# Making gathered columns on VectorE alone instead of on VectorE and ScalarE: a graph attention kernel on one core

## The chip, the core and the metric

The kernel runs on one core of one Trainium2 chip. A core has TensorE (PE; its weight loads are shown apart, as PEld), VectorE (DVE), ScalarE (ACT), GpSimd (POOL) and SyncE (SP), which run their own instruction streams and meet at semaphores, and 16 DMA engines that serve the queues of all of them. The metric is the device time of one execution in microseconds; the lower the better. The time before is the median of three runs, 2430.73 us.

## The reference

A graph layer with 6250 nodes, 206250 edges sorted by destination, width 128 and 8 heads of 16, then a residual and a layer norm:

```python
Qh = (h @ WQ).reshape(N, H, D)
Kh = (h @ WK).reshape(N, H, D)
Vh = (h @ WV).reshape(N, H, D)
Eh = (edge_attr @ WE).reshape(-1, H, D)
score = jnp.einsum('ehd,ehd,ehd->eh', Kh[src], Qh[dst], Eh) * inv_sqrt_d
score = jnp.exp(jnp.clip(score, -5.0, 5.0))
msg = Vh[src] * score[:, :, None]
wV = jax.ops.segment_sum(msg, dst, num_segments=N)
Z = jax.ops.segment_sum(score, dst, num_segments=N)
h_out = wV / (Z[:, :, None] + 1e-06)
...
x = _layernorm(x + h_out, axis=-1)
```

The sources of the edges are random nodes, so the rows `Kh[src]`, `Vh[src]` have to be fetched row by row. The destinations are sorted, so neighbouring edges add into neighbouring nodes.

## The kernel before

The edges are cut into 1612 tiles of 128, and the tiles into 406 batches of four (the last few of two or one). A table `kv` of the K and V rows of all nodes is computed once and stored in HBM; x itself lies transposed in SBUF (`xT_sb`, a feature per partition and a node per column), interleaved with a zero behind each node in `xz`.

For each batch the loop does, spread over some five iterations:

- `gather`: POOL fetches the K and V rows of a tile's 128 sources with one indirect DMA per tile (line 463), into `kvrows`. The first gather of a batch waits for the qps of an earlier batch, twelve batches back at first and three later on (`lag`).
- `stage_a`: TensorE makes Q rows of the destinations (`qps`, line 560, from a one-hot matrix) and the edge features (`eps`, line 565).
- `products` and `scores`: VectorE multiplies `kvrows` by `qps` (line 572) and by `eps` (line 574), and sums by head (lines 581, 584).
- `weigh` and `messages`: ScalarE takes the exponentials (lines 590, 592), and VectorE multiplies the V rows by them (line 623).
- `stage_0`, `stage_0t` with `mark`, `mark_t`: TensorE and ScalarE build the one-hot matrices of the destinations (`marks`, lines 508 and 529; `marks_t`, lines 542 and 551).
- `stage_c`: TensorE adds the messages by destination (`agg`, line 645); `finish` and `layernorm` finish blocks of nodes when all their edges are in. `q_rows` (lines 313 to 320) builds the table of Q rows a little ahead of its use.

Not every tile is gathered. In 169 batches the last of the four tiles is made another way: the 128 source columns of x are copied from `xT_sb` into a tile `xcol` in SBUF, one by one, at addresses that are read into registers 16 at a time (`addresses`, line 389); then TensorE multiplies `xcol` by the K and V weights (`colkv`, line 445), and ScalarE puts the result into `kvrows` (line 452). `gather` leaves these tiles out. Which batches have such a tile is fixed by `COL0` and `COLP`: from batch 26 on, five in eleven.

The copies of a tile are shared. ScalarE makes the first 58 of the 128 columns, one per instruction (line 421). VectorE makes the other `COLV` = 70, two per instruction (line 418): it reads eight bytes at each of two places, where one pair is (column, zero) and the other (zero, column), and joins them with a bitwise or. The copies are spread evenly over the batches, eight batches ahead of their use (`due`, `COLL`). VectorE's come in runs of eight instructions, at two places of a batch (`run`), with two halves between which other small work is put; ScalarE's come all in one place, after `place_columns`, and ahead of `mark` and `mark_t` (`columns`).

The part of the loop in which the engines' orders are fixed (lines of the order in one iteration):

```python
place_columns()
if 0 <= b - 1 < nbat:
    stage_0(b - 1)
if b + 2 < nbat:
    stage_0t(b + 2)
if b < nbat:
    columns(b)
mark(b - 1)
if b + 2 < nbat:
    mark_t(b + 2)
```

All instructions of an engine run in the order in which the program issues them. `marks`, `qrows`, `colkv` and the sums of `finish` share two PSUM buffers; `marks_t`, `qps` and `eps` have one each.

Of the kernel before, what the change touches and what calls it, by code (L numbers as in the profile page):

```python
# [8 lines left out]
F32 = mybir.dt.float32  # L9
I32 = mybir.dt.int32  # L10
# [15 lines left out]
LEFT, RIGHT = 1, 1  # L26
# [24 lines left out]
QLOOK = 3  # L51
QREG = 16
COL0 = 26
COLP = (11,5)
COLN = 16
COLV = 70
COLL = 8
RING = 4096
MR = 3 * WT + 2
# [2 lines left out]
XT_AT = RING + P  # L62
# [21 lines left out]
def col_runs(v):  # L84

    n = len(column_tiles()) * (P - COLV, COLV)[v]
    return -(-n // (COLN * P))


def column_runs(srcT, v):  # L90

    import numpy as np
    cols = srcT.reshape(NT, P)[column_tiles()]
    cols = (cols[:, :P - COLV], cols[:, P - COLV:])[v].ravel()
    runs = np.zeros((col_runs(v) * P, COLN), cols.dtype)
    runs.ravel()[:len(cols)] = cols
    return np.ascontiguousarray(runs.reshape(col_runs(v), P, COLN).transpose(1, 0, 2).reshape(P, -1))


def pair_of(t):  # L100
# [14 lines left out]
def q_built(j):  # L115

    return min(NB, (j * N // NJ + 3 * P - 1) // P)


@with_exitstack  # L120
def edge_attention(ctx: ExitStack, tc: tile.TileContext, x, xT, srcT, srcA, srcV, dstT, dstB, dst0, bnd, loB, onB, onQ, eaT,
                   wq, wkv, we, out, kv, qtab, qs, relD, relO):
    nc = tc.nc
    cp = ctx.enter_context(tc.tile_pool(name="const", bufs=1))
# [25 lines left out]
    batches = cut_batches()  # L150
    nbat = len(batches)
    col_batches = [t // B for t in column_tiles()]
    col_at = [cp.tile([P, col_runs(v), COLN], I32, name=f"col_at{v}") for v in range(2)]

    def src_col(t):
        return src_sb[0][:, t:t + 1] if t < C0 else src_sb[1][:, t - C0:t - C0 + 1]

    with ExitStack() as fast:
# [225 lines left out]
        def addresses(v):  # L384

            while len(ahead[v]) < 2 and read[v] < len(col_batches) * share[v]:
                r = read[v] // COLN
                read[v] += COLN
                ahead[v].append(nc.values_load_multi_w_load_instructions(  # L389
                    col_at[v][r % P:r % P + 1, r // P],  # L390
                    engines=((mybir.EngineType.Activation, mybir.EngineType.DVE)[v],),
                    min_val=XT_AT + 8 * LEFT - 4, max_val=XT_AT + 8 * (LEFT + N - 1),
                    skip_runtime_bounds_check_because="edges name nodes")[1])

        def column(at, n, dt):
# [3 lines left out]
            return xz_bytes[:, ds(at - XT_AT, n)].bitcast(dt)  # L399
# [6 lines left out]
        def copy(v):  # L406

            c, (k, i) = copied[v] % COLN, divmod(copied[v], share[v])
            if c == 0:
                addresses(v)  # L410
                at_hand[v] = ahead[v].pop(0)
            copied[v] += 1 + v
            if k not in col_tiles:
                col_tiles[k] = wp.tile([P, P], F32, name="xcol", bufs=6)
            to, at = col_tiles[k], at_hand[v]
            if v:
                i += share[0]
                nc.vector.tensor_tensor(to.bitcast(I32)[:, i:i + 2], column(at[c], 8, I32),  # L418
                                        column(at[c + 1], 8, I32), op=ALU.bitwise_or)
            else:  # L420
                nc.scalar.copy(to[:, i:i + 1], column(at[c], 4, F32))  # L421
# [95 lines left out]
        def mark(b):  # L517

            if b not in marks:
                return  # L520
            m, oh, h, n, k = marks.pop(b)
            base = oh[:, h, :n, HW * h:HW * h + HW]
            if k == 2:
                (p_, *dims) = [list(x) for x in base.ap]
                base = bass.AP(tensor=base.tensor, offset=base.offset, ap=[p_, [B * P + HW, 2], *dims])
                m = m.rearrange("p (k b) w -> p k b w", k=2)
            else:
                m = m[:, :n]
            nc.scalar.activation(base, m, AF.Relu)  # L529
# [3 lines left out]
        def stage_0t(b):  # L533

            if b in marks_t or b in ohTs:
                return
            t0, n = batches[b][0], len(batches[b])
            m = psM.tile([QROWS, B * P], F32, name="marks_t")
            for i in range(0, n * P, WT * P - t0 % WT * P):
                e0 = (t0 * P + i) % (WT * P)  # L540
                w = min(n * P - i, WT * P - e0)
                nc.tensor.matmul(m[:, i:i + w], steps_q, rels[(t0 * P + i) // (WT * P)][:, e0:e0 + w], start=True, stop=True)  # L542
            marks_t[b] = m, n
# [154 lines left out]
        for b in range(nbat + 4):  # L698
# [41 lines left out]
            for _ in run(b, 0.5) if on else ():  # L740
                fill(False)
# [3 lines left out]
            for _ in run(b, 1.0) if on else ():  # L745
                fill()
# [225 lines left out]
```

## Time and profile before

| | |
|---|---|
| median of three runs | 2430.73 us (2430.68 to 2443.36) |
| the profiled execution | 2453.43 us, of which its span 2451.6 us |
| mean granted TensorE clock | 0.771 |
| DMA | 329.11 MB, mean 134 GB/s |
| gathers in the trace (line 463) | 1395 from `kv`, 48 from x |
| column copies in the trace | ScalarE 9802, VectorE 5915 |

The profile page shows one execution. In its groups of instructions each row has the line, the engine, the operation, what is written and read, the count, then the busy time and the mean of one in ns, and then the idle time of the engine ahead of them with what ended most of it. "issue" is idle time for which the profile shows no cause, "remote" a release whose origin it doesn't show. In a timeline each row has the start, the duration, the engine and line, the count of merged instructions, and in brackets the idle time ahead of it. Spans on POOL are rough by the page's own words, and the ends of matmuls are modelled.

### The profile page before, as it was taken

The page shows a single profiled execution, that of the slowest core. Times are in us where ns is not written, and L with a number is a line of the kernel's source. Part 1 is how long each engine was busy: PE and PEld are TensorE (multiplying, and loading weights), DVE is VectorE, ACT ScalarE, POOL GpSimd, SP SyncE. Part 2 cuts the span into 40 slices and gives each one's busy share as a digit, 9 for nine tenths or more (in the row PEclk, how much of TensorE's full clock was granted, in tenths as well). Part 3 has the DMA queues.
Part 4 walks back from the last instruction along what each step waited for, and adds up shares of the span by engine and source line. Part 5 has one row for each costly group of instructions (what it writes and reads, how often), then busy time and mean ns, then how long its engine had stood idle before and what let it go on. Part 6 is the DMA issues. An engine that isn't in the chain of part 4 may idle for free.

```text
span 2451.6 us, 47432 instructions
## 1 busy us (share of the span) xinstructions
PE 1827.4 (75%) x10000; PEld 1470.7 (60%) x10000; DVE 1672.0 (68%) x8773; ACT 1567.2 (64%) x11614; POOL 1377.3 (56%) x1450
## 2 busy tenths in 40 slices
PE   5786677777777778688777777777777777767786
PEld 3565555655556656566556666666655656556565
DVE  3455676676677767677767677777677777676765
ACT  2334666666677767676766766767676766666752
POOL 6554555555555555555655555655555655555563
PEclk7777777687788877777878777877777877777877
DMA  6544444344344444444444444544444444445442
GB/s 201 183 140 120 120 123 125 112 145 130 111 138 146 129 123 149 120 138 130 149 133 130 142 145 123 153 134 127 138 139 125 138 138 132 144 120 149 136 130 62
DMA packets 165518, 329.11 MB, mean 134 GB/s; under 512 B 65389, under 2 KB 90929, under 8 KB 165221
## 3 DMA queue, kind: packets, MB, share of 16 engines
q0 software_dynamic: 68480, 186.02, 26.1%
q1 hardware_dynamic: 95617, 139.22, 18.1%
q14 instruction: 217, 1.78, 0.2%
q8 instruction: 80, 1.31, 0.2%
q10 hardware_dynamic: 1124, 0.79, 0.1%
HBM read 309.01 MB, written 16.88 MB: 133 GB/s over the span
## 4 chain that ended last, share of the span: by engine, by line
PE 29%; ACT 24%; DVE 18%; issue 13%; another core or an unknown queue 7%; DVEq 4%; ACTq 2%; DMA 1%; POOL 0%; SPq 0%; POOLq 0%
ACT xcol L421 16%; PE eps L565 8%; PE agg L645 7%; DVE xcol L418 5%; DVEq L389 4%; DVE kq L574 3%; DVE kq L572 3%; PE finps L604 3%; ACT onehotT L551 3%; PE marks_t L542 3%; PE qps L560 2%; DVE sc L581 2%; ACT onehot L529 2%; DVE msg L623 2%
## 5 line engine op out<-in xcount | busy, mean ns | idle before, releaser
L463 POOL DMA_INDIRECT kvrows<-kv,src x1395 | 1326.5, 951 | 1032.2 <-issue 334.2
L421 ACT COPY xcol<-xz 128x1 f32 x9802 | 1046.2, 189 | 401.7 <-issue 389.9
L645 PEld LDWEIGHTS agg<-msg,onehot 128*128 128x128 f32 x3224 | 529.4, 241 | 382.5 <-issue 220.4
L565 PE MATMUL eps<-we_sb,ea 128*128 128x128 f32 x3224 | 592.3, 341 | 216.5 <-DVE kq L574 181.9
L565 PEld LDWEIGHTS eps<-we_sb,ea 128*128 128x128 f32 x3224 | 519.8, 244 | 249.2 <-DVE kq L574 205.3
L645 PE MATMUL agg<-msg,onehot 128*128 128x136 f32 x3224 | 621.2, 349 | 26.9 <-DVE msg L623 8.4
L418 DVE TENSOR_TENSOR xcol<-xz 128x2 int32 x5915 | 508.8, 152 | 143.8 <-issue 139.7
L574 DVE TENSOR_TENSOR kq<-kq,eps 128x512 f32<-128x512 f32 x406 | 272.4, 671 | 295.3 <-remote 177.8
L572 DVE TENSOR_TENSOR kq<-kvrows,qps 128x512 f32<-128x512 f32 x406 | 275.4, 678 | 184.8 <-PE qps L560 46.2
L542 PE MATMUL marks_t<-rows_q,steps_q 5*126 5x512 bf16 x406 | 190.4, 469 | 228.1 <-ACT onehotT L551 79.3
L623 DVE TENSOR_TENSOR msg<-kvrows,exp_p 128x512 f32<-128x512 f32 x406 | 273.1, 673 | 10.4 <-ACT exp_p L590 8.3
L581 DVE TENSOR_REDUCE sc<-kq 128x32 f32<-128x512 f32 x406 | 272.4, 671 | 0.3
L551 ACT ACTIVATE onehotT<-marks_t 126x512 bf16<-126x512 f32 x406 | 237.1, 584 | 46.2 <-remote 22.2
L590 ACT ACTIVATE exp_p<-sc 128x32 f32<-128x32 f32 x406 | 81.8, 202 | 238.6 <-DVE msg L623 105.0
L560 PE MATMUL qps<-qw,onehotT 126*128 126x128 bf16 x1612 | 194.5, 254 | 21.2 <-DVE kq L572 13.9
L560 PEld LDWEIGHTS <-onehotT 126*128 126x128 bf16 x1612 | 155.9, 117 | 71.4 <-issue 43.7
L604 PEld LDWEIGHTS finps<-sum,shift 128*128 128x128 f32 x640 | 116.8, 270 | 57.8 <-issue 24.7
L445 PE MATMUL colkv<-wkv_sb,xcol 128*128 128x256 f32 x338 | 136.1, 494 | 18.9 <-ACT onehot L529 10.4
L604 PE MATMUL finps<-sum,shift 128*128 128x136 f32 x640 | 129.5, 376 | 11.4 <-remote 6.7
L529 ACT ACTIVATE onehot<-marks 128x512 f32<-128x512 f32 (+2 forms) x206 | 119.4, 580 | 15.2 <-issue 6.4
L592 ACT ACTIVATE msg<-sc 128x32 f32<-128x32 f32 x406 | 88.1, 217 | 6.1 <-issue 6.0
L508 PE MATMUL marks<-steps,rows 26*128 26x512 bf16 (+2 forms) x206 | 91.9, 446 | 0.0
(86 smaller groups left out, 822.1 us busy)
## 6 DMA issues: line engine op xcount, KB each, us to landing
ea<-eaT SPq DMA_DIRECT2D x201, 512.0 KB
kvrows<-kv,src POOLq DMA_INDIRECT x1395
qw<-qs SPq DMA_DIRECT2D x202, 31.5 KB
kv<-ea SPq DMA_DIRECT2D x12, 512.0 KB
qs<-qst SPq DMA_DIRECT2D x48, 96.0 KB
rows_q<-relD SPq DMA_DIRECT2D x202, 6.0 KB
rows<-relO SPq DMA_DIRECT2D x202, 6.0 KB
xb<-x SPq DMA_DIRECT2D x24, 128.0 KB
```

The lines of the kernel that those rows point to most:

```text
L418: nc.vector.tensor_tensor(to.bitcast(I32)[:, i:i + 2], column(at[c], 8, I32), column(at[c + 1], 8, I32), op=ALU.bitwise_or)
L421: nc.scalar.copy(to[:, i:i + 1], column(at[c], 4, F32))
L463: ins = nc.gpsimd.indirect_dma_start(out=g[:k, i, :f], out_offset=None, in_=rows, in_offset=bass.IndirectOffsetOnAxis(ap=src_col(t)[:k], a ...
L551: nc.scalar.activation(ohTs[b][:, :n * P], m[:, :n * P], AF.Relu)
L560: expanded[b] = nc.tensor.matmul(pq[:, i, :], ohT[:, i * P:i * P + P], loaded[t0 // WT], start=True, stop=True)
L565: nc.tensor.matmul(pe[:, i, :], ea[:, i * P:i * P + P], we_sb, start=True, stop=True)
L572: nc.vector.tensor_tensor(t0[:, :n], g[:, :n, :D], pq[:, :n], op=ALU.mult)
L574: nc.vector.tensor_tensor(t0[:, :n], t0[:, :n], pe[:, :n], op=ALU.mult)
L581: nc.vector.tensor_reduce(sc[:, :n], t0[:, :n].rearrange("p b (h d) -> p b h d", h=H), axis=AX.X, op=ALU.add)
L604: nc.tensor.matmul(ps, shift[:, P - s:2 * P - s], sums[k // 2][:, k % 2], start=first and i == 0, stop=stop and i == len(parts) - 1)
L623: nc.vector.tensor_tensor(m[:, :n, :D].rearrange("p b (h d) -> p b h d", h=H), g[:, :n, D:].rearrange("p b (h d) -> p b h d", h=H), exp_p[ ...
L645: nc.tensor.matmul(aggs[u][:, 0 if final else k % 2], oh[:, i, :], m[:, i, :], start=not final and t % (2 * G) == 0, stop=tail)
```

## The change

ScalarE copies no columns any more. VectorE makes all 128 columns of a tile, two per instruction as before, and there are 83 such tiles instead of 169 (`COLP` is 9 and 2: two batches in nine). So 86 tiles more are gathered by POOL. There is one table of addresses instead of two, `columns` and its call are gone, and `due` and `run` count the columns of whole tiles. The order of everything else in the loop is the same.

```diff
-COLP = (11,5)
+COLP = (9, 2)
 COLN = 16
-COLV = 70
 COLL = 8
...
-        copied, projected = [0, 0], []
-        share = [P - COLV, COLV]
-        ahead, read, at_hand = [[], []], [0, 0], [None, None]
+        copied, projected = [0], []
+        total = len(col_batches) * P
+        ahead, read, at_hand = [], [0], [None]
...
-        def due(b, v, part):
-
-            n = int((b + part - 1 - COL0 + COLL) * COLP[1] * share[v] / COLP[0] + 1e-6) // (1 + v) * (1 + v)
-            return min(n, len(col_batches) * share[v])
+        def due(b, part):
+
+            return min(int((b + part - 1 - COL0 + COLL) * COLP[1] * P / COLP[0] + 1e-6) // 2 * 2, total)
...
-            if v:
-                i += share[0]
-                nc.vector.tensor_tensor(to.bitcast(I32)[:, i:i + 2], column(at[c], 8, I32),
-                                        column(at[c + 1], 8, I32), op=ALU.bitwise_or)
-            else:
-                nc.scalar.copy(to[:, i:i + 1], column(at[c], 4, F32))
-
-        def columns(b, part=1.0):
-
-            while copied[0] < due(b, 0, part):
-                copy(0)
+            at = at_hand[0]
+            nc.vector.tensor_tensor(col_tiles[k].bitcast(I32)[:, i:i + 2], column(at[c]),
+                                    column(at[c + 1]), op=ALU.bitwise_or)
 
         def run(b, part):
 
-            left = due(b, 1, part) - copied[1]
-            if left >= COLN // 2 or 0 < left == len(col_batches) * share[1] - copied[1]:
+            left = due(b, part) - copied[0]
+            if left >= COLN // 2 or 0 < left == total - copied[0]:
                 for i in range(COLN // 2):
                     if i == COLN // 4:
                         yield
-                    if copied[1] < len(col_batches) * share[1]:
-                        copy(1)
+                    if copied[0] < total:
+                        copy()
...
-        for v in range(2):
-            nc.sync.dma_start(col_at[v], (srcA, srcV)[v].rearrange("p (r c) -> p r c", c=COLN))
-            nc.vector.tensor_scalar(col_at[v], col_at[v], 8, XT_AT + 8 * LEFT, op0=ALU.mult, op1=ALU.add)
-        odd = col_at[1].rearrange("p r (c z) -> p (r c) z", z=2)[:, :, 1]
+        nc.sync.dma_start(col_at, srcC.rearrange("p (r c) -> p r c", c=COLN))
+        nc.vector.tensor_scalar(col_at, col_at, 8, XT_AT + 8 * LEFT, op0=ALU.mult, op1=ALU.add)
+        odd = col_at.rearrange("p r (c z) -> p (r c) z", z=2)[:, :, 1]
...
-            if b < nbat:
-                columns(b)
             mark(b - 1)
```

More of the change, by code (lines that the diff above doesn't have):

```diff
@@ L81, in column_tiles, with col_runs, column_runs @@
     return [batches[b][-1] for b in at if b < len(batches) and batches[b][-1] < NT - TAIL - 4 * B]
[L84 to L90, printed above, removed]
+def col_runs():
+    return -(-len(column_tiles()) // COLN)
+def column_runs(srcT):
     import numpy as np
-    cols = srcT.reshape(NT, P)[column_tiles()]
-    cols = (cols[:, :P - COLV], cols[:, P - COLV:])[v].ravel()
-    runs = np.zeros((col_runs(v) * P, COLN), cols.dtype)
+    cols = srcT.reshape(NT, P)[column_tiles()].ravel()
+    runs = np.zeros((col_runs() * P, COLN), cols.dtype)
     runs.ravel()[:len(cols)] = cols
-    return np.ascontiguousarray(runs.reshape(col_runs(v), P, COLN).transpose(1, 0, 2).reshape(P, -1))
+    return np.ascontiguousarray(runs.reshape(col_runs(), P, COLN).transpose(1, 0, 2).reshape(P, -1))
 def pair_of(t):
@@ L152, in edge_attention @@
     col_batches = [t // B for t in column_tiles()]
-    col_at = [cp.tile([P, col_runs(v), COLN], I32, name=f"col_at{v}") for v in range(2)]
+    col_at = cp.tile([P, col_runs(), COLN], I32, name="col_at")
     def src_col(t):
@@ L378, in edge_attention @@
         used = [0]
-        copied, projected = [0, 0], []
-        share = [P - COLV, COLV]
-        ahead, read, at_hand = [[], []], [0, 0], [None, None]
[L384 to L391, printed above, removed]
+        copied, projected = [0], []
@@ L392, in addresses, with column @@
+        total = len(col_batches) * P
+        ahead, read, at_hand = [], [0], [None]
+        def addresses():
+            while len(ahead) < 2 and read[0] < total:
+                r = read[0] // COLN
+                read[0] += COLN
+                ahead.append(nc.values_load_multi_w_load_instructions(
+                    col_at[r % P:r % P + 1, r // P], engines=(mybir.EngineType.DVE,),
                     min_val=XT_AT + 8 * LEFT - 4, max_val=XT_AT + 8 * (LEFT + N - 1),
                     skip_runtime_bounds_check_because="edges name nodes")[1])
-        def column(at, n, dt):
+        def column(at):
@@ L397, in column @@
             at = at.with_bounds(min_val=XT_AT + 8 * LEFT - 4, max_val=XT_AT + 8 * (LEFT + N - 1),
                                 guaranteed_mod_val=0, out_of_modulus=4)
-            return xz_bytes[:, ds(at - XT_AT, n)].bitcast(dt)
-        def due(b, v, part):
-            n = int((b + part - 1 - COL0 + COLL) * COLP[1] * share[v] / COLP[0] + 1e-6) // (1 + v) * (1 + v)
-            return min(n, len(col_batches) * share[v])
-        def copy(v):
-            c, (k, i) = copied[v] % COLN, divmod(copied[v], share[v])
+            return xz_bytes[:, ds(at - XT_AT, 8)].bitcast(I32)
@@ L409, in copy @@
+        def due(b, part):
+            return min(int((b + part - 1 - COL0 + COLL) * COLP[1] * P / COLP[0] + 1e-6) // 2 * 2, total)
+        def copy():
+            c, (k, i) = copied[0] % COLN, divmod(copied[0], P)
             if c == 0:
-                addresses(v)
-                at_hand[v] = ahead[v].pop(0)
-            copied[v] += 1 + v
+                addresses()
+                at_hand[0] = ahead.pop(0)
+            copied[0] += 2
             if k not in col_tiles:
                 col_tiles[k] = wp.tile([P, P], F32, name="xcol", bufs=6)
-            to, at = col_tiles[k], at_hand[v]
@@ L941 @@
         "srcT": np.ascontiguousarray(srcT.reshape(NT, P).T),
-        "srcA": column_runs(srcT, 0),
-        "srcV": column_runs(srcT, 1),
+        "srcC": column_runs(srcT),
         "dstT": np.ascontiguousarray(dstT.reshape(NT, P).T),
```

2 lines of the change are left out of this document (1 added, 1 removed).

## The prediction

> **What bounds the kernel now.** I read the page first, for the shares of the engines, the chain of work and the costliest groups.
>
> ```profile
> span 2451.6 us, 47432 instructions
> ...
> PE 1827.4 (75%) x10000; PEld 1470.7 (60%) x10000; DVE 1672.0 (68%) x8773; ACT 1567.2 (64%) x11614; POOL 1377.3 (56%) x1450
> ...
> PE 29%; ACT 24%; DVE 18%; issue 13%; another core or an unknown queue 7%; DVEq 4%; ACTq 2%; DMA 1%; POOL 0%; SPq 0%; POOLq 0%
> ...
> L463 POOL DMA_INDIRECT kvrows<-kv,src x1395 | 1326.5, 951 | 1032.2 <-issue 334.2
> L421 ACT COPY xcol<-xz 128x1 f32 x9802 | 1046.2, 189 | 401.7 <-issue 389.9
> ...
> L418 DVE TENSOR_TENSOR xcol<-xz 128x2 int32 x5915 | 508.8, 152 | 143.8 <-issue 139.7
> ...
> L445 PE MATMUL colkv<-wkv_sb,xcol 128*128 128x256 f32 x338 | 136.1, 494 | 18.9 <-ACT onehot L529 10.4
> ```
>
> The view of line 463 adds the gathers from x, ahead of the table kv.
>
> ```profile
> L463 POOL DMA_INDIRECT kvrows<-x,src x48: 939/945/2613, 3.7 to 71.2; - x48
> ```
>
> No engine is full, POOL is not on the chain that ended last, and it looks idle for 44% of the span: a gather shows 951 ns, and mostly some 0.3 us of issue before the next. The timeline of POOL alone says otherwise. I take it at the end, where no column is copied any more (ScalarE's last copy starts at 2376.2, VectorE's at 2372.4).
>
> ```profile
> L421 ACT COPY xcol<-xz x9802: 173/187/213, 202.4 to 2376.2; 128x1 f32 x197
> ...
> L418 DVE TENSOR_TENSOR xcol<-xz x5915: 118/151/235, 196.7 to 2372.4; 128x2 int32 x198
> ```
>
> ```profile
> 2377.03 0.95 POOL L463 DMA_INDIRECT kvrows<-kv,src  x1 [2.01 <-PE qps L560]
> ...
> 2383.04 0.95 POOL L463 DMA_INDIRECT kvrows<-kv,src  x1 [1.31 <-PE marks_t L542]
> ...
> 2393.37 0.94 POOL L463 DMA_INDIRECT kvrows<-kv,src  x1 [1.88 <-remote]
> ...
> 2405.18 0.94 POOL L463 DMA_INDIRECT kvrows<-kv,src  x1 [2.08 <-PE marks_t L542]
> ```
>
> The same in stretches (stretch, length, POOL's busy time in gathers and their number, granted clock, DMA share, GB/s):
>
> ```profile
> 2377.00:2419.90 42.90, 27.46 (x29) 0.82 0.36 103
> 200.00:2377.00 2177.00, 1229.67 (x1295) 0.77 0.45 133
> ```
>
> Between the starts shown POOL makes 4, 7 and 8 gathers, back to back. The runs take 6.01, 10.33 and 11.81 us from start to start, and the idle time behind them grows with their length: 1.31, 1.88, 2.08 us. A wait for another engine would not grow with the number of gathers; work of POOL that goes on behind the recorded end of the instruction would. So a gather costs POOL 42.90/29 = **1.48 us**, not 1.25. From 200 to 2377 us, where columns are copied, POOL issues 1295 gathers in 2177 us, 1.68 us each. At 1.48 they would take 1917 us: POOL's own work is 88% of that stretch, and 260 us are waits of POOL for the loop.
>
> Next, who holds the loop up. Each gather group waits for a qps of TensorE some batches back, so I read a long POOL wait with all engines.
>
> ```profile
> 1384.38 0.69 DVE L574 TENSOR_TENSOR kq<-kq,eps 128x512 f32<-128x512 f32 x1 [1.95 <-remote]
> ...
> 1384.66 0.95 POOL L463 DMA_INDIRECT kvrows<-kv,src  x1 [0.30 <-issue]
> ...
> 1385.78 0.19 ACT L421 COPY xcol<-xz 128x1 f32 x1 [0.52 <-issue]
> 1386.49 0.19 ACT L421 COPY xcol<-xz 128x1 f32 x1 [0.52 <-issue]
> 1387.20 1.58 ACT L421 COPY xcol<-xz 128x1 f32 x15 [0.51 <-issue]
> 1388.68 0.59 ACT L529 ACTIVATE onehot<-marks 128x512 f32<-128x512 f32 x1
> ...
> 1389.32 0.80 PE L313 MATMUL qrows<-wq_sb,xz 128*128 128x128 f32 x2 [3.76 <-ACT onehot L529]
> ...
> 1389.91 0.63 PE L560 MATMUL qps<-qw,onehotT 126*128 126x128 bf16 x4
> ...
> 1390.82 0.94 POOL L463 DMA_INDIRECT kvrows<-kv,src  x1 [5.21 <-PE qps L560]
> ```
>
> Another one, where a run of gathers holds the others up:
>
> ```profile
> 1734.29 1.16 PE L565 MATMUL eps<-we_sb,ea 128*128 128x128 f32 x8
> ...
> 1740.02 0.95 POOL L463 DMA_INDIRECT kvrows<-kv,src  x1 [0.30 <-issue]
> ...
> 1741.13 0.69 DVE L574 TENSOR_TENSOR kq<-kq,eps 128x512 f32<-128x512 f32 x1 [3.87 <-remote]
> ```
>
> Late in a run of gathers ScalarE's copies, else about 0.1 us apart, come one or two per 0.7 us, and engines resume together as the run ends: L574 of VectorE, whose eps TensorE issued from 1734.29 on, waits 3.87 us until 1741.13, just behind the recorded end of that run's last gather (1740.02 + 0.95). So the loop advances mostly at the start of a run and after it. In the first of the two waits the last gather ends at 1385.61; of the 5.21 us that follow, 1.88 are POOL's own (the run of 7 above), and 3.3 are excess. In those, ScalarE first works off its 15 remaining copies (1387.20 to 1388.68, 1.5 us); only then come onehot, qrows, qps and the gather.
>
> So POOL's gathers set the pace, and ScalarE's copies are a part, not all, of what POOL waits for on top.
>
> **The change part by part.**
>
> *Gathers.* 1612 tiles less 169 are the 1395 + 48 gathers of the trace; less 83 they are 1529, so **86 more**. The steps between the runs above give (10.33 - 6.01)/3 = 1.44 and 11.81 - 10.33 = 1.48 us for one more in a run; I take 1.47: 86 x 1.47 = **+126 us**. Bounds: below, 86 x 1.25 = 107 us, which is nothing if it fits into POOL's waits (a rival); above, 86 x 1.68 = +145 us, if the loop's waits grow in step. Nothing covers this term, since POOL has no spare time at 1.48 us. The added bytes are 6% of queue 0's, and the DMA engines are 45% busy in the stretch; I cost them at nothing.
>
> The Trainium skill (Perfetto Trace Analysis, section DMA Instruction — SWDGE (GPSIMD)) says that the profile's end of such an instruction is the moment when the last DSP has finished generating descriptors. By that rule POOL is free 0.95 us after a start, and the growing idle time would be other engines' doing; the rows above speak against it.
>
> *ScalarE's columns.* 9802 copies go, 1046.2 us busy and 401.7 us of idle before them, with ScalarE's register loads; of that only what POOL's waits contain comes back. Who waits for ScalarE is in the waits of TensorE:
>
> ```profile
> PE marks_t L542 <- ACT onehotT L551: 79.3, 55, 7.8
> ...
> PE marks_t L542 <- ACT exp_p L590: 28.3, 27, 2.0
> PE marks_t L542 <- ACT kvrows L452: 26.8, 15, 3.5
> ...
>   ACT onehot L529: 65.1, 25
> ```
>
> (the last: idle time before qrows, L313, of loads and matmuls together, so about half of it counts once). 79.3 + 28.3 + 26.8 + 33 = 167 us is what TensorE waits for a ScalarE that is behind, and is my upper bound of the gain: some of it lies under POOL's own 88%. The lower bound is nothing. In the wait shown ScalarE has 1.5 of 3.3 us; in others the chain runs through VectorE's msg or a half-clock agg, and copies lie beside it. I take a third of 260 us: **-87 us**. What is late next is VectorE's chain L574, L581, its column run, L584, L623, which stays as it is.
>
> *VectorE's columns.* 83 x 64 = 5312 instructions for 5915, 603 fewer at (508.8 + 139.7)/5915 = 110 ns: 66 us of VectorE's time. Per batch it makes 128 x 2/9 = 28 columns where it made 70 x 5/11 = 32. VectorE sits on POOL's path only in the excess, 260 of 2177 us, an eighth: -8 us, within the rounding of the term above, so not added. The cover is POOL; without it the whole 66 us would count.
>
> The Trainium skill (SBUF — State Buffer, section Who interferes with whom) says that a VectorE instruction with two SBUF inputs contends with a GpSimd instruction that reads SBUF; such are these column instructions, so 603 fewer might shorten gathers. A gather lasts 0.94 to 0.95 us in the rows with columns and without, so I give it nothing.
>
> *Projections.* 86 pairs of colkv go, 136.1 x 86/169 = 69 us of TensorE, and 86 copies L452; like VectorE's, they count in the excess alone, an eighth, and are left in the rounding. The address table is one short load and one multiply less at the start: nothing, beside the first gathers.
>
> *Sum.* +126 - 87 = **+39 us**. The profiled execution took 2453.4 us (span 2451.6), 0.9% over the median of 2430.7; the difference carries over, so 2430.7 + 39 = **2470 us**.
>
> **The rivals.**
>
> *Faster: the loop catches up.* ScalarE's backlog is the main cause of POOL's excess, and without it the loop always has its qps ready. At the end of the span, without any columns, three runs go at POOL's own price. If TensorE's whole 167 us come back, 2430.7 + 126 - 167 = **2390 us**; with all 260 us of waits gone 2297, the extreme. It decides from the point where more than 126 us are saved, half of POOL's excess. For it: the wait shown. Against it: VectorE still makes 14 column instructions a batch, and longer runs hold the loop up for longer.
>
> *Full price: nothing comes back.* Longer runs of POOL hold the others up as much as ScalarE's absence helps: +145, **2576 us**. For it: the runs of seven are the ones with the long waits behind them, and four-gather batches become the rule (323 of 406, before 237).
>
> *The gathers are hidden and the loop is the bound*, as POOL's 56% and its 0% of the chain suggest; then the change does not cost what it adds, and 167 us come off: **2264 us**. POOL at 1.25 us a gather would be busy for 1529 x 1.25 = 1911 us only. (The rule of the Trainium skill on the profile's end, above, would have it so.) Against it: the 4, 7, 8 pattern.
>
> That the change doesn't do what it says is excluded by the counts: nothing else makes columns.
>
> **How the numbers follow.** Less than 0.5%, 12 us, is about what a measurement of this kernel can't tell from no change. Forecast (between +12 and +110 us) 0.53; full price (above +110) 0.14; the two sides cancel within 12 us 0.10; faster, loop catches up 0.20; gathers hidden 0.03. So slower 0.67, same 0.10, faster 0.23. The range leaves out the hidden gathers, the outer part of the rival of catching up and that of the full price: 2375 to 2565.
>
> **What would show it.** In the changed kernel's page: 1481 gathers on L463 from kv; no L421-like copies on ScalarE, and ScalarE busy for some 1567 - 1046 = 521 us. If the first step is right, POOL's runs of 4 take about 6.0 us from start to start, and the mean per gather in the long stretch lies between 1.48 and 1.68 us; I expect about 1.60. If it falls to 1.48, the faster rival holds; if it stays at 1.68, the full price. If runs of 4 come closer than 5.6 us, POOL's own price is wrong. If waits for ScalarE vanish from marks_t and qrows while POOL's mean stays, the second step is wrong: VectorE or the hold-up itself sets the excess.

## The result, and the profile after

Before takes 2448.45 us and after 2426.59 us, medians of 20 runs each taken side by side (2429.1 to 2466.73, and 2414.82 to 2439.95). The ratio is 0.9919, 95% interval 0.9894 to 0.9943: after is some 20 us faster. Forecast were 2470 us, 39 us slower than before; the range of 2375 to 2565 us holds the time, the sign does not hold.

Of the seven lots of runs below, the first two had every execution of every kernel some 20% shorter, before's own too (medians of 1887.94 and 1889.46 us), so each ratio is taken to before in the same lot; the result and the other five lots have before at 2417 to 2467 us. I call them the short and the long lots and come back to them at the end.

The page of after: the busy times of the engines, the chain that ended last, and the two groups that grew or shrank.

```profile
span 2419.9 us, 35774 instructions
...
PE 1823.0 (75%) x9828; PEld 1470.2 (61%) x9828; DVE 1637.7 (68%) x8169; ACT 580.7 (24%) x1726; POOL 1458.4 (60%) x1536
...
PE 9%; DVE 6%; issue 3%; another core or an unknown queue 1%; DVEq 1%; POOL 0%; DMA 0%; SPq 0%; ACT 0%; POOLq 0%; ACTq 0%
...
L449 POOL DMA_INDIRECT kvrows<-kv,src x1481 | 1408.3, 951 | 920.1 <-issue 359.8
...
L411 DVE TENSOR_TENSOR xcol<-xz 128x2 int32 x5312 | 467.5, 154 | 133.4 <-issue 126.2
```

The 86 gathers are there (1481 for 1395), ScalarE's 9802 copies are gone (ACT 580.7 us busy for 1567.2; 521 were forecast), and yet POOL sits idle less than before: 920.1 us ahead of its gathers where it was 1032.2. The chain is followed back over only a fifth of the span here and carries nothing. In the view of groups most of TensorE's waits for ScalarE have gone as well. marks_t, which waited 79.3 us for ScalarE's onehotT, waits 3.8 us:

```profile
L528 PE MATMUL marks_t<-rows_q,steps_q 5*126 5x512 bf16 x406 | 196.9, 485 | 21.5 <-issue 14.8 <-ACT onehotT L537 3.8 <-DMA rows<-relO 2.7
```

The same stretch as in the prediction, POOL alone (stretch, length, busy time and number of gathers, granted clock, DMA share, GB/s):

```profile
200.00:2377.00 2177.00, 1334.20 (x1406) 0.74 0.47 140
```

That is 2177/1406 = 1.55 us for a gather, where 1.68 were before and 1.60 forecast. By the prediction's own price of 1.48, POOL's waits for the loop would have shrunk from 260 to 96 us: 164 us would have come back, not 87. The experiments show that this way of dividing the time was itself wrong.

**A way to divide it that the experiments bear out.** Between two gathers of a run POOL is idle for 0.305 us (0.30 or 0.31 in the timelines; 451.2/1481 in a run of the second lot below that has no longer pauses). So I take the idle time that the group's row gives, less 0.305 us for each gather, and call the rest the gaps: before 1032.2 - 1395 x 0.305 = 607 us, after 920.1 - 1481 x 0.305 = 468 us. At 0.951 + 0.305 = 1.256 us, 86 gathers are +108 us; the gaps are -138 us; the sum of -30 us is, but for 2 us, the difference of the two spans, 2451.6 and 2419.9. That alone is bookkeeping; that 1.256 us is what a gather costs, and that the gaps belong to the loop, is for the runs to show.

### The profile page after: what moved, and what is told of

Its sections match the earlier page's. It is cut to its first block, busy times and chain, and to the rows that moved or that the text cites. A ratio compares the mean times of both kernels' runs of the same rounds, so it can differ in the third digit from the quotient of the medians.

```text
span 2419.9 us, 35774 instructions
## 1 busy us (share of the span) xinstructions
PE 1823.0 (75%) x9828; PEld 1470.2 (61%) x9828; DVE 1637.7 (68%) x8169; ACT 580.7 (24%) x1726; POOL 1458.4 (60%) x1536
## 3 DMA queue, kind: packets, MB, share of 16 engines
q0 software_dynamic: 72608, 197.30, 27.7%
## 5 line engine op out<-in xcount | busy, mean ns | idle before, releaser
L449 POOL DMA_INDIRECT kvrows<-kv,src x1481 | 1408.3, 951 | 920.1 <-issue 359.8
L551 PE MATMUL eps<-we_sb,ea 128*128 128x128 f32 x3224 | 622.2, 352 | 299.0 <-DVE kq L560 182.2
L551 PEld LDWEIGHTS eps<-we_sb,ea 128*128 128x128 f32 x3224 | 541.8, 253 | 344.7 <-DVE kq L560 207.2
L631 PE MATMUL agg<-msg,onehot 128*128 128x136 f32 x3224 | 634.6, 354 | 107.4 <-DVE msg L609 47.8
L631 PEld LDWEIGHTS agg<-msg,onehot 128*128 128x128 f32 x3224 | 540.4, 245 | 276.3 <-DVE msg L609 92.8
L411 DVE TENSOR_TENSOR xcol<-xz 128x2 int32 x5312 | 467.5, 154 | 133.4 <-issue 126.2
L528 PE MATMUL marks_t<-rows_q,steps_q 5*126 5x512 bf16 x406 | 196.9, 485 | 21.5 <-issue 14.8
L494 PE MATMUL marks<-steps,rows 26*128 26x512 bf16 (+2 forms) x206 | 98.6, 479 | 0.0
L314 DVE CAST qst<-qrows 128x128 bf16<-128x128 f32 (+1 forms) x49 | 14.2, 290 | 116.6 <-remote 67.8
L570 DVE TENSOR_SCALAR sc<-sc 128x32 f32<-128x32 f32 x406 | 76.6, 189 | 15.4 <-remote 6.6
```

What stands on the lines that cost most here:

```text
L411: nc.vector.tensor_tensor(col_tiles[k].bitcast(I32)[:, i:i + 2], column(at[c]), column(at[c + 1]), op=ALU.bitwise_or)
L449: ins = nc.gpsimd.indirect_dma_start(out=g[:k, i, :f], out_offset=None, in_=rows, in_offset=bass.IndirectOffsetOnAxis(ap=src_col(t)[:k], a ...
L551: nc.tensor.matmul(pe[:, i, :], ea[:, i * P:i * P + P], we_sb, start=True, stop=True)
L631: nc.tensor.matmul(aggs[u][:, 0 if final else k % 2], oh[:, i, :], m[:, i, :], start=not final and t % (2 * G) == 0, stop=tail)
```

## The experiments

Two theories stood at the start. **A**: gathers set the pace, and ScalarE's column copies made a good part of POOL's waits. **B**: the gathers are covered, and after is faster because an engine of the loop has less to do. Within A, **A1** blames the place of the copies in ScalarE's queue, **A2** their load. **C**, added later: what is held up during runs of gathers makes the waits, whatever ScalarE does. Some expectations speak of two kinds of chip; but by the records the same chip ran the first lot, a short one, and the fifth, a long one.

### First lot (short): four changes

One column tile in place of 83:

```diff
-    return [batches[b][-1] for b in at if b < len(batches) and batches[b][-1] < NT - TAIL - 4 * B]
+    return [batches[b][-1] for b in at if b < len(batches) and batches[b][-1] < NT - TAIL - 4 * B][:1]
```

> After with one column tile instead of 83: 82 more tiles are gathered (1563) and VectorE loses almost all its column copies. Theory A (POOL's queue of gathers sets the time: gathers x 1.48 us and the waits of POOL for the loop on top): 82 x 1.48 = 121 us more POOL work; of after's 95 us of waits some more may go, since VectorE is freed too. So 40 to 121 us over after, i.e. +1% to +4% against the kernel before. Theory B (the gathers are covered, the loop's engines set the time, and after is faster because an engine of the loop has less to do): no slower than after, 1% faster than before or better.

Before, with one wide copy for ScalarE's 58 of a tile:

```diff
-            if c == 0:
+            if c == 0 and v:
...
-            else:
-                nc.scalar.copy(to[:, i:i + 1], column(at[c], 4, F32))
+            elif i == 0:
+                nc.scalar.copy(to[:, :share[0]], xT_sb[:, LEFT:LEFT + share[0]])
```

> Before, with ScalarE's 58 copies of one column per tile replaced by one copy of 58 neighbouring columns (58 columns of each of the 169 tiles are then not those of the edges), without the address loads of ScalarE. The 169 tiles stay, 1395 gathers stay. Theory A: the gathers' own 1395 x 1.48 us stay, and the waits of POOL for the loop fall from 260 us to after's level of 95 us: about 165 us faster, -5.5% to -7.5%. Theory B (gathers covered, ScalarE's load alone is what after took away): the same gain as after, about -1%.

After, with ScalarE's copies put back into a tile `scratch`:

```diff
+            while extra[0] < min(int((b - COL0 + COLL) * 5 * 58 / 11 + 1e-6), 169 * 58):
...
+                nc.scalar.copy(scratch[:, c:c + 1], xz_bytes[:, ds(at - XT_AT, 4)].bitcast(F32))
...
+            if b < nbat:
+                columns(b)
             mark(b - 1)
```

> After, with before's 58 x 169 one-column copies of ScalarE and their address loads put back at their old place in its queue, into a tile that nobody reads (the output stays that of the reference). 1481 gathers as in after. Theory A: the waits of POOL return, 165 us more than after: 2580 us or so, +5% to +7% against before. Theory B: back at before's time, within 1% of it.

Before, with the copies moved in ScalarE's queue:

```diff
-            if b < nbat:
-                columns(b)
             mark(b - 1)
...
                 if ready:
                     finish(ready.pop(0))
+            if b < nbat:
+                columns(b)
```

> Before, with ScalarE's column copies of a batch moved behind the batch's masks (mark, mark_t) and the finish in its queue; nothing removed. Theory A1 (the waits come from the place: the copies stand ahead of the one-hot copies that the gathers' offsets and the sums wait for): most of the 165 us go with 169 tiles kept, -3% to -7%. Theory A2 (the waits come from the load, wherever it stands: during a run of gathers ScalarE gets through only one copy in 0.7 us, so 58 copies in 2.2 batches are late anyway and hold the next batch's work): within 1.5% of before. Theory B: within 1% of before.

| first lot, before 1887.94 us | us | to before, 95% |
|---|---|---|
| one column tile | 2051.71 | 1.087 (1.085 to 1.090) |
| one wide copy | 1872.10 | 0.991 (0.988 to 0.995) |
| ScalarE's copies back in after | 1950.12 | 1.034 (1.031 to 1.036) |
| copies behind masks and finish | 1874.09 | 0.992 (0.989 to 0.995) |

A's sizes did not come out as written, since before itself took 1888 us. B's size for the wide copy (about -1%) and the sizes of A2 and B for the moved copies (within 1.5% and 1%) did, but B's reason did not, since one column tile is 8.7% slower. The page of the run with one column tile says why:

```profile
L449 POOL DMA_INDIRECT kvrows<-kv,src x1563 | 1487.5, 952 | 478.4 <-issue 350.6
```

478.4 us of idle time for 1563 gathers is 0.306 us each: no gaps at all. A gather every 1.258 us makes up 1966 us of the span of 2052. The two runs at 1481 and 1563 gathers differ by 101.6 us, 1.24 us for each of 82. Here the gathers are in no way hidden, against B, and ScalarE has next to nothing to hold up: its copies cost 16 us in before and, as the next lot shows, nothing in after.

### Second lot (short): after itself, and three again

> After itself, beside before, on the chip of these runs: the first four runs went to a chip on which before takes 1888 us, and where a gather takes 1.254 us from start to start with hardly a longer gap between any two. Theory A there: time = 1.26 us x gathers whenever POOL never waits, as in the runs with 1481 and 1563 gathers (1950 and 2052 us): after 1950 us, +3.3% against before, although it leaves out 9802 copies of ScalarE. Theory B (time follows the load of the loop's engines): faster than before, as on the chip of the first profiles. If the chip is the one of the first profiles (before about 2440): 2420 to 2440 us, -0.9%, with some 200 gaps of POOL over 0.4 us between 200 us and the end.

> Before with one wide copy of ScalarE for the 58 of a tile (58 columns of these tiles are not those of the edges). On a chip with before at 2440 us: Theory A -5.5% to -7.5% (165 us of POOL's waits gone, gathers as before); Theory B about -1%. On a chip with before at 1888 us: about -1% again, since POOL waits there for no more than some 50 us in all.

> After with before's one-column copies of ScalarE put back, into a tile that nobody reads. On a chip with before at 2440 us: Theory A +5% to +7% against before; Theory B within 1%. On a chip with before at 1888 us: +3.3% again, the same as after, because POOL never waits in either.

> Before with ScalarE's column copies moved behind the masks and the finish of their batch. On a chip with before at 2440 us: Theory A1 (the place in ScalarE's queue makes the waits) -3% to -7%; Theory A2 (the load makes them, wherever it stands) within 1.5%. On a chip with before at 1888 us: about -1% again.

After takes 1951.42 us here, 1.032 times before (1.029 to 1.036), as A had it; with ScalarE's copies put back 1951.33; the wide copy 1873.08 and the copies moved behind 1874.04, both 0.992. So in the short lots **the same change makes the kernel 3.2% slower**, and 9802 copies of ScalarE put back into after cost nothing. The page of after in this lot:

```profile
L449 POOL DMA_INDIRECT kvrows<-kv,src x1481 | 1409.7, 952 | 451.2 <-issue 336.7
```

451.2 us are 1481 x 0.305: no gaps. This kernel takes 475 us less here than in the result, and the gaps there are 468 us.

### Third lot (long): before once more

> Before itself, for its trace on the chip of these runs, on which after is 62 us slower. There 86 gathers more at 1.254 us are 108 us, so by Theory A POOL waits for the loop for 108 - 62 = 46 us in all in before, against some 2 us in after: its gaps over 0.4 us between gathers come to 40 to 55 us from 200 us on (630 us on the chip of the first profiles), and most end on qps or marks_t, behind ScalarE's copies. Theory B: no such gaps, the difference comes from elsewhere. On a chip where before takes 2440 us: gaps of some 630 us again.

It was meant for a short lot and fell into a long one: 2438.5 us, idle time 1018.0 us ahead of 1395 gathers, so gaps of 592 us. It tells nothing of the question asked, and is a single run; it repeats before's profile in another lot.

### Fourth lot (long): is it ScalarE's copies, and is it their place?

The same two kernels, on before at 2416.96 us.

> Before with one wide copy of ScalarE in place of the 58 of a tile, without its address loads (58 columns of these tiles are not those of the edges). On a chip where before takes some 2440 us, Theory A1 or A2 (ScalarE's copies made 165 us of POOL's waits): -5.5% to -7.5% against before. Theory C (the waits come from handshakes that are held up during runs of gathers, whatever ScalarE does; after gains by VectorE's or the batches' part): within 1.5%. On a chip where before takes 1888 us: -0.9% as in the two runs there.

> Before with ScalarE's column copies moved behind the masks and the finish of their batch, nothing removed. On a chip where before takes some 2440 us: Theory A1 (their place in the queue) -3% to -7%; Theory A2 (their load) within 1.5%; Theory C within 1%. On a chip where before takes 1888 us: -0.8% as in the two runs there.

The wide copy takes 2309.64 us, 0.955 of before (0.950 to 0.960): 107 us less, with all 1395 gathers. Moving the copies behind takes 2445.22 us, 1.013 (1.008 to 1.017): slower. The groups of the first, with the gaps at 892.5 - 1395 x 0.305 = 467 us:

```profile
L463 POOL DMA_INDIRECT kvrows<-kv,src x1395 | 1328.8, 953 | 892.5 <-issue 328.7 <-PE qps L560 115.9 <-PE marks_t L542 92.7
...
L542 PE MATMUL marks_t<-rows_q,steps_q 5*126 5x512 bf16 x406 | 188.6, 464 | 11.4 <-issue 6.8 <-ACT onehotT L551 2.2 <-DMA rows<-relO 1.7
```

And the waits of TensorE in the second (in all, times, longest):

```profile
PE eps L565 <- DVE kq L574: 243.3, 120, 6.5
...
PE finps L604 <- ACT kvrows L452: 29.5, 10, 6.2
PE marks_t L542 <- ACT onehotT L551: 26.1, 25, 4.3
```

ScalarE's copies hold POOL up (against C, which had the wide copy within 1.5%), but not just because they stand ahead of the masks (against A1): behind them, marks_t waits for onehotT 26.1 us in place of 79.3, and finps waits for ScalarE instead. Added up over all rows of the view, TensorE's waits for ScalarE fall from 232 to 135 us, those for VectorE grow from 248 to 355, and POOL's gaps stay, 1022.2 - 1395 x 0.305 = 597 us for 607. So it is the load (A2), though 107 us of it and not the 165 expected; only this one other place was tried. The 467 us of gaps that stay with the wide copy have another cause, which C may name.

### Fifth lot (long): the terms one by one

All four are after with one thing added or taken, on before at 2446.5 us. The unread gathers:

```diff
                 if b in col_batches and i == B - 1:
+                    idle = gp.tile([P, 2 * D], F32, name="idle", bufs=4)
+                    nc.gpsimd.indirect_dma_start(
+                        out=idle[:, :f], out_offset=None, in_=rows,
+                        in_offset=bass.IndirectOffsetOnAxis(ap=src_col(t)[:k], axis=0))
                     continue
```

> After itself, as the foot of the two differences below. Where before takes some 2440 us: -0.8% against before (between -0.3% and -1.3%); where it takes 1888 us: +3.2%.

> After with before's 9802 one-column copies of ScalarE and their address loads back at their old place, into a tile that nobody reads. Where before takes some 2440 us: the run without these copies at 169 tiles was 108 us below before. Theory A (ScalarE's copies make POOL wait, at any number of gathers): 80 to 130 us over after, +2.5% to +4.5% against before. Theory C (after gained by its other parts): less than 30 us over after. Where before takes 1888 us: the same as after.

> After with one column tile instead of 83, so 82 gathers more and almost none of VectorE's column copies. Where before takes some 2440 us: at the prediction's price of 1.47 us a gather 121 us over after; at the net price that the difference of after and of the run without ScalarE's copies gives (89 us for 86 gathers and 603 fewer instructions of VectorE, 1.04 us each) 85 us over after or less, since VectorE loses 5248 instructions more. Where before takes 1888 us: 102 us over after, as before.

> After with a gather for each of its 83 column tiles as well, into a buffer that nobody reads, so that each batch has all four gathers and VectorE still makes its columns. Where before takes some 2440 us: at 1.47 us each 122 us over after; at 1.25 us (start to start within a run, if a gather added to a run makes no new gap) 104 us; by the rival that a gather hides in waits that are there anyway under 50 us. What it takes over the run with one column tile is what VectorE's copies cost at an equal load of POOL: 0 if POOL's gaps are not VectorE's. Where before takes 1888 us: 104 us over after, and the same as with one column tile.

| fifth lot, before 2446.5 us | us | to before, 95% | over after | gaps of POOL, us |
|---|---|---|---|---|
| after | 2428.23 | 0.993 (0.990 to 0.996) | | 937.9 - 1481 x 0.305 = 486 |
| ScalarE's copies back | 2528.40 | 1.034 (1.026 to 1.042) | +100.2 | 1027.9 - 1481 x 0.305 = 576 |
| one column tile, 82 gathers more | 2482.54 | 1.010 (1.004 to 1.017) | +54.3 | 906.1 - 1563 x 0.305 = 429 |
| 83 unread gathers | 2530.85 | 1.032 (1.027 to 1.038) | +102.6 | 932.0 + 25.3 - 1564 x 0.305 = 480 |

The idle times stand in the groups of the four runs. After:

```profile
L449 POOL DMA_INDIRECT kvrows<-kv,src x1481 | 1407.4, 950 | 937.9 <-issue 363.1 <-remote 129.6 <-PE qps L546 99.8
```

ScalarE's copies back, where marks_t waits for ScalarE again (259.0 us idle in all):

```profile
L467 POOL DMA_INDIRECT kvrows<-kv,src x1481 | 1405.0, 949 | 1027.9 <-issue 364.3 <-PE qps L564 194.9 <-remote 124.4
...
L546 PE MATMUL marks_t<-rows_q,steps_q 5*126 5x512 bf16 x406 | 197.2, 486 | 259.0 <-ACT scratch L440 112.6 <-ACT onehotT L555 82.0 <-ACT msg L596 15.3
```

One column tile:

```profile
L449 POOL DMA_INDIRECT kvrows<-kv,src x1563 | 1484.7, 950 | 906.1 <-issue 389.9 <-remote 151.5 <-PE marks_t L528 87.5
```

The unread gathers, in two rows:

```profile
L453 POOL DMA_INDIRECT kvrows<-kv,src x1481 | 1407.0, 950 | 932.0 <-issue 362.6 <-remote 146.1 <-PE qps L550 89.5
...
L447 POOL DMA_INDIRECT idle<-kv,src x83 | 78.5, 946 | 25.3 <-issue 21.0 <-DVE sc L574 2.7 <-DVE h L862 0.6
```

83 gathers alone cost 102.6/83 = **1.24 us each** and leave the gaps as they are, 486 and 480 us. At 1.47 us each they would cost 122 us, and no two single runs, one of each kernel, are more than 116 us apart. ScalarE's copies cost 100 us, 90 of them in the gaps. At an equal load of POOL (one gather apart), VectorE's 5248 column instructions with their 82 projections cost 2530.85 - 2482.54 = 48 us, 51 of them in the gaps, 0.59 us a tile. The intervals are some 13 to 20 us wide on either side, so the sums of gaps, which agree with the differences of times to 10 us, carry much of this.

### Sixth lot (long): more tiles by VectorE alone

```diff
-COLP = (9, 2)
+COLP = (3, 1)
...
-                for i in range(COLN // 2):
+                for i in range(COLN // 2 * max(1, min(2, left // COLN))):
```

and the same with `(11, 5)`. The first makes 124 tiles, as its 7936 column instructions of 64 a tile show (its label says 112), and the second 169.

> After with one column tile in three batches instead of two in nine, all by VectorE (runs of 8 or 16 instructions): some 41 tiles more are made of columns and fewer gathered. Where before takes some 2440 us: a gather alone costs 1.24 us there, a tile of VectorE's columns (48 us for 82) 0.59 us, so 0.65 us are saved for each: 25 us under after, about -1.8% against before. By the rival that VectorE's time counts in full (64 x 110 ns = 7 us a tile, as the prediction had it without POOL's cover) it is slower than after. Where before takes 1888 us: POOL alone sets the time, 1.25 us for each gather less, +0.5% to +1.5% against before.

> After with before's 169 column tiles, all 128 columns of each by VectorE: 1395 gathers as in before. Where before takes some 2440 us: at 0.65 us saved for each of 86 tiles 56 us under after, about -3% against before, if VectorE's price stays as it is; VectorE's busy time grows by 86 x 64 x 88 ns = 484 us to some 2100 us, so the rival is that it becomes the bound, and the time is above after's. Where before takes 1888 us: VectorE's 2100 us are more than the 1888 us, and it is the bound: +10% or more.

With before at 2418.11 us, 124 tiles take 2458.47 us (1.016; 1.012 to 1.021) and 169 tiles 2719.10 us (1.127; 1.122 to 1.132). A flat price of VectorE is refuted: neither beats after, and it is the rival that holds. In the run with 169 tiles POOL's waits for qps alone are 647.6 us. VectorE is busy for 76% of the span, but 480.4 us of its idle time stand ahead of its column instructions, with no other engine named; between these, its queue issues 1352 loads of addresses, which are not counted as busy. With them it is taken for 2054.5 + 480.4 = 2535 of 2715.3 us, 93%, where after has 1637.7 + 126.2 = 1764 of 2419.9, 73%:

```profile
PE 1973.7 (73%) x10000; PEld 1581.2 (58%) x10000; DVE 2054.5 (76%) x13673; ACT 584.4 (22%) x1812; POOL 1376.4 (51%) x1450
...
L411 DVE TENSOR_TENSOR xcol<-xz 128x2 int32 x10816 | 925.1, 154 | 485.8 <-issue 480.4 <-PE marks_t L528 0.3
...
L449 POOL DMA_INDIRECT kvrows<-kv,src x1395 | 1327.2, 951 | 1297.6 <-PE qps L546 647.6
```

After at 0.9925 (the mean of its two ratios) would be 2400 us in this lot. With a gather at 1.24 us, a tile of VectorE's costs 0.59 us up to 83 of them, (58 + 41 x 1.24)/41 = 2.7 us from there to 124, and (260.6 + 45 x 1.24)/45 = 7.0 us from there to 169. The last is 64 instructions at 110 ns: the full time of VectorE, the price that the prediction named for the case without POOL's cover. Both runs also have column runs of up to 16 instructions where after has 8, and no run tells apart how much of the rise is due to that.

### Seventh lot (long): copies or their address loads

The wide copy again, with the line `if c == 0:` left as in before, so that ScalarE still loads all its addresses.

> Before with one wide copy of ScalarE in place of the 58 of a tile, as in the run that gained 4.5%, but with all of ScalarE's address loads kept (58 columns of these tiles are not those of the edges). If the copies themselves make the waits of POOL: -3.5% to -5% against before. If the register loads of 16 addresses (some 1 us each in ScalarE's queue, 613 of them) make them: within 1.5% of before. Between the two, both have a part. If before takes some 1890 us in this run: -0.9%, and nothing is told apart.

2331.37 us on before at 2422.53, 0.962 (0.959 to 0.965): 91 us less. The copies themselves make most of the waits; some 16 us are left for the 613 loads (107 less 91, from different lots, which is hardly more than the noise).

## Why the prediction was wrong, point by point

**Gathers, +126 us: mis-sized, by a wrong reading.** The prediction held that the idle time behind a run of gathers is POOL's own work, because it grows with the run (1.31, 1.88, 2.08 us), and so put a gather at 1.48 us and an added one at 1.47. In many runs of after the pattern is still there. A piece of its timeline, and what the other engines do in the longest of the runs:

```profile
1381.10 0.94 POOL L449 DMA_INDIRECT kvrows<-kv,src  x1 [1.31 <-PE qps L546]
...
1387.27 0.94 POOL L449 DMA_INDIRECT kvrows<-kv,src  x1 [1.48 <-PE qps L546]
...
1397.73 0.94 POOL L449 DMA_INDIRECT kvrows<-kv,src  x1 [2.01 <-DVE xcol L411]
...
1401.91 1.98 PE L551 MATMUL eps<-we_sb,ea 128*128 128x128 f32 x8
...
1403.34 0.16 DVE L873 TENSOR_TENSOR w<-w,vh 128x2 f32<-128x2 f32 x1
...
1406.48 0.94 POOL L449 DMA_INDIRECT kvrows<-kv,src  x1 [0.30 <-issue]
1408.50 0.69 DVE L560 TENSOR_TENSOR kq<-kq,eps 128x512 f32<-128x512 f32 x1 [5.00 <-remote]
...
1409.21 0.60 ACT L515 ACTIVATE onehot<-marks 128x512 f32<-128x512 f32 x1 [5.74 <-remote]
...
1409.61 0.94 POOL L449 DMA_INDIRECT kvrows<-kv,src  x1 [2.19 <-remote]
```

Here a run of four takes 6.17 us and one of eight 11.88. But "what would show it" held POOL's own price to be wrong if runs of four come closer than 5.6 us, and some do. Call it a run when no pause in it is over 0.36 us: from 200 us on, after has 54 runs of four, and six take less, the shortest 5.07 us; even before has five such among 124. With one column tile in the fifth lot, 74 of 113 runs of eight take less than the 11.81 us of the prediction's run of eight. The shortest of each kind, with the pause behind it in the last row:

```profile
1329.47 0.95 POOL L449 DMA_INDIRECT kvrows<-kv,src  x1 [2.03 <-remote]
...
1334.54 0.94 POOL L449 DMA_INDIRECT kvrows<-kv,src  x1 [0.38 <-PE qps L546]
```

```profile
1791.94 0.94 POOL L449 DMA_INDIRECT kvrows<-kv,src  x1 [2.25 <-PE marks_t L528]
...
1802.25 0.94 POOL L449 DMA_INDIRECT kvrows<-kv,src  x1 [0.40 <-remote]
```

POOL can start again 0.38 us after four gathers and 0.40 us after eight, so the 1.31 and 2.08 us are not its own work. Two more findings say the same: in the short lots the same instructions follow each other for the whole kernel without any such idle time, and in a long lot 83 more of them leave its sum unchanged. An added gather goes into a run that is there anyway and costs 102.6/83 us: for 86 **+106 us**. The argument that a wait for others could not grow with the run was wrong: in the rows above VectorE and ScalarE stand still for 5.00 and 5.74 us of the run of eight and go on 1.1 and 1.8 us after its last gather has ended (1406.48 + 0.94). What VectorE needs there, TensorE's eps, had ended at 1403.89 by the profile. Why the pause is mostly longer behind a longer run was not found.

The Trainium skill (Perfetto Trace Analysis, section DMA Instruction — SWDGE (GPSIMD)) puts the profile's end of a gather where the last DSP has generated its descriptors. The prediction set this aside; the 0.30 us from one gather's end to the next agree with it, and the growing idle time was not POOL's own work after all. That gathers are hidden, which the prediction tied to this rule, did not follow.

**ScalarE's columns, -87 us: right in kind, too small.** Taken away at 169 tiles they give 107 us, put back into after they cost 100 us. The bound of 167 us from TensorE's waits held as a number, but it left out rows: all of TensorE's waits for ScalarE come to 232 us in before. In the wide copy they fall to 41 us while its waits for VectorE grow from 248 to 341, so such a sum is no measure of what comes back. That the term came near was partly luck: the 260 us of POOL's waits were 2177 - 1295 x 1.256 = 550 us of gaps in the same stretch, and 107 us are under a fifth of them, not the third that was chosen by a wait in which ScalarE had 1.5 of 3.3 us.

**VectorE's columns and the projections, put at nothing: too small.** The run with ScalarE's copies put back differs from before by the 86 gathers, 603 fewer instructions of VectorE and 86 fewer projections (and by the fact that nothing waits for what ScalarE copies), and is 82 us above it; less 106 us for the gathers, **-24 us** are left. Between after and the wide copy, from two lots, it is (0.9925 - 0.9552) x 2417 = 90 us, less 106: -16 us. No run took them alone, and the noise of these differences (the first has an interval of 20 us to either side) is about as large as they are, so what makes the -24 us stays open. But the price of VectorE's tiles rises steeply just there, 0.59 to 2.7 us, so an eighth of its busy time, which is 8 us, may be a poor measure.

**The sum.** +106 - 100 - 24 = -18 us, the difference of after and before in the fifth lot (it closes by construction, since the -24 is a remainder). Against +126 - 87 = +39 the three terms are off by 20, 13 and 24 us, all to the same side; the first was a wrong mechanism, the others sizes. No one of them turns the sign: with the first put right the sum is +19 us, with the second too +6, and only the third, the remainder, makes it negative. Of the rivals, "the loop catches up" has the outcome: 138 us of gaps are gone, more than the 108 us of gathers, and the 1.55 us per gather lies between the 1.60 forecast and the 1.48 that it asked for. Its reason holds in part only, since ScalarE's copies make under a fifth of the gaps (107 of 607 us) and not most of them. "Full price" had nothing coming back, and 138 us of gaps did; "gathers hidden" is refuted by the unread gathers, at 1.24 us each.

**A version that beats both** was not found for the long lots: 1, 124 and 169 tiles of VectorE are all slower than after's 83. In the short lots the moved copies beat both kernels (0.992, where after is at 1.032), but they lose 1.3% in the long ones.

## What to carry to other kernels

Before idle time behind a run of instructions is taken for their own work, look for the shortest pause behind such a run in the whole trace, which the engine's own work could not undercut; then add some of the instructions, unread, and see whether the sum of gaps changes. An engine that is busy for two thirds of the span can still be near its limit: 41 tiles more cost VectorE's path 2.7 us each where the 83 before cost 0.6 (in longer column runs), so a price taken at one load is not carried to another. And where a change trades a fixed cost for waits, its sign hangs on whether those waits exist on the day: here it turned from 0.992 to 1.032.

## What was not expected of the hardware

The same kernel has two speeds hundreds of microseconds apart, by lots and not by single runs: after took 1951.42 us in one and 2428.23 in another, before 1887.94 and 2446.5 on the very same chip. What differs is the hold-up. At the same time in the short lot's timeline (a later batch, since it runs faster), VectorE goes from instruction to instruction while gathers are issued, and a gather that needs qps has it in time:

```profile
1405.57 0.95 POOL L449 DMA_INDIRECT kvrows<-kv,src  x1 [0.30 <-DVE msg L609]
...
1406.40 0.16 DVE L873 TENSOR_TENSOR w<-w,vh 128x2 f32<-128x2 f32 x1
1406.48 0.68 DVE L560 TENSOR_TENSOR kq<-kq,eps 128x512 f32<-128x512 f32 x1
1406.82 0.95 POOL L449 DMA_INDIRECT kvrows<-kv,src  x1 [0.30 <-PE qps L546]
```

The gathers last the same in both (L449 952 and 951 ns), VectorE's kq nearly so (0.68 and 0.69 us here); TensorE's matmuls are longer at the lower granted clock (eps 319 ns at 0.857, 352 at 0.745). What grows in these rows is the time from one engine's end to another's start during a run of gathers. What makes a lot long was not found. It isn't the chip, and nothing in the kernels differs. Nor is it the granted clock alone: one column tile in the first lot had no gaps at 0.796, and the wide copy in the fourth 467 us of them at 0.801. The packets of the queue that the gathers use took the same time in after in both, 27.7% of 2419.9 us and 34.2% of 1950.6, about 670 us.
